# Masked attention: one more block of each group summed by an accumulating transfer, with resized tile pools

## The chip, the core and the metric

The kernel runs on one core of a Trainium2 chip. A core has TensorE (PE in the profile: matrix products and transposes), VectorE (DVE), ScalarE (ACT), GpSimd (POOL) and SyncE (SP), which issue in order, each from its own queue, and wait for each other by semaphores; 16 DMA engines move data. [...] The metric is the device time of one execution in microseconds (us), the median of several runs.

## The reference

Eight independent inputs (F = 8) of N = 2048 rows and C = 256 channels pass one attention layer with H = 8 heads of D = 32, under one mask adj, then layer norms and a small MLP:

```python
q, k, v = split(x @ w_qkv)                              # per head: [f, h, n, 32]
scores  = einsum('fnhd,fmhd->fhnm', q, k) / sqrt(32)
scores  = where(adj > 0, scores, -1e9)
attn    = softmax(scores, axis=-1)                      # exp(scores) / sum over m
t       = einsum('fhnm,fmhd->fnhd', attn, v)
y = layernorm(x + t); y = layernorm(y + mlp(y)); out = layernorm(x + y)
```

Everything is float32. Two sums over m (the keys) are wanted for every query and head: the sum of exp(score) times v, and the sum of exp(score) itself, the denominator. This document is about how the second is made.

## The kernel before

**Groups and slots.** The queries of an input are cut into four chunks of 512 (`qc`), the heads into two sets of four (`g`), the keys into 16 blocks of 128 (`mb`). A group is one `(f, qc, g)`; there are 8 x 4 x 2 = 64. One step of the main loop, here called a slot, handles one block of one group, so a group has 16 slots, the kernel has 1024, and one input ("frame") has 128. In slot t the loop issues, in this order:

- `advance(t)`: side work from the list `fill` (below);
- `exponentials(t+1)`: ScalarE turns the masked scores of the next block into exponentials in place (L237), a tile `p` of 128 x 2048 floats, that is 1 MB;
- `scores(t+2)`: TensorE computes the scores of the block after that (L230: four products of 32 rows each, side by side), and VectorE adds the mask on the way from PSUM into a new tile `p` (L233, two instructions);
- `values(t)`: TensorE multiplies block t's exponentials by v (L249), adding up in one PSUM bank over the 16 blocks;
- `add_up(t)`: the block is added to a partial sum for the denominator.

**The denominator.** Within a group the 16 tiles are reduced to four before TensorE sees them. Blocks 3, 6, 8, 11, 13, 15 are added into block 0's tile by GpSimd (L271, the list `POOLED`). Blocks 4, 7, 10 are added into block 1's tile and blocks 5, 9, 12 into block 2's by DMA transfers that read, add and write in SBUF (L268, the two chains of `MOVED`); GpSimd issues them, and before each it waits for the previous one of its chain to have landed. Block 14 (`ALONE`) stays as it is. `denominator` then multiplies each of the four tiles ("terms") by a matrix of ones (L310), one term at a time, in the order block 14, chain 1, chain 2, pooled; the PSUM result is the sum over keys. The last term is not issued before slot `t + SUM` (t = the group's last slot, SUM = 4). In the very last group blocks 13 and 15 are terms of their own (`ENDED`).

**Side work.** `denominator`, the projections (`project`: k and v of the next input, `ask`: its queries), transposes (`turn`) and the layer norms and MLP (`outcome`, `tail`, `feed_forward`) are Python generators in the list `fill`, with a start slot and a due slot. `advance` resumes them at build time: each slot earns 2200 units of credit (`STEP`), a product of four columns of 512 costs 2048, and the next piece is let in when the credit has 1024 (`UNIT`) or the piece is due. Most slots so carry one piece of side work on TensorE, between the values of one slot and the scores of the next; some carry two or none. `NEXT` lists, by slot of the frame, when the projections of the following work are started. All of it is one fixed program: the order on each engine is settled when it is built.

**Tile pools.** `pp` holds the 1 MB tiles `p` (11 of them), `kp` and `vp` the k and v tiles (12 each, a quarter of the size; 8 are in use for one input, the rest is room for the next), `qp` the query tiles (6). A new tile takes the buffer that was released first: in both programs, in nearly every group, the buffer of the new group's block 2 is that of block 10 of the group before (with 11 buffers) or of block 9 (with 12), and so on. VectorE's write at L233 waits for that release: for a block added by a transfer, until the transfer has landed; for one added by GpSimd, until the add is done; for a term, until its product with ones is done.

Of the kernel before, what the change touches and what calls it, by code (L numbers as in the profile page):

```python
# [61 lines left out]
def fast_path(ctx, tc, cst, x, adj, out, RS):  # L62
    nc = tc.nc
    F, N, C = x.shape
    NCK, TPC, MB = N // CH, CH // P, N // P
# [2 lines left out]
    dp = ctx.enter_context(tc.tile_pool(name="dp", bufs=1, space=bass.MemoryType.DRAM))  # L68
    mkp = ctx.enter_context(tc.tile_pool(name="mkp", bufs=MB // 2 + 1))
    ld = ctx.enter_context(tc.tile_pool(name="ld", bufs=LD))  # L70
    kp = ctx.enter_context(tc.tile_pool(name="kp", bufs=3 * NCK))
    qp = ctx.enter_context(tc.tile_pool(name="qp", bufs=6))
    vp = ctx.enter_context(tc.tile_pool(name="vp", bufs=3 * NCK))
    pp = ctx.enter_context(tc.tile_pool(name="pp", bufs=11))
    work = ctx.enter_context(tc.tile_pool(name="work", bufs=1))
    yp = ctx.enter_context(tc.tile_pool(name="yp", bufs=2))
    op = ctx.enter_context(tc.tile_pool(name="op", bufs=1))
# [14 lines left out]
    def transposes(ps, src, ident=ident):  # L92
        state["credit"] -= TURN
        for j, s in enumerate(src):
            nc.tensor.transpose(ps[:, j * P:(j + 1) * P], s, ident)
# [6 lines left out]
    def bank(dt=F32):  # L102
        shape = [P, CH] if dt == F32 else [P, 2, CH]
        if state["side"] is not None:
            i = 1 - state["side"]
            return ps_x[i].tile(shape, dt, name=f"x{i}")
        i = state["turn"]
        state["turn"] = (i + 1) % 5
        pool = ps_s[i] if i < 3 else ps_x[i - 3]
        return pool.tile(shape, dt, name=f"s{i}" if i < 3 else f"x{i - 3}")  # L110
# [4 lines left out]
    def take(shape, dt):  # L115
        live.pop(0)
        live.append(ld.tile(shape, dt, name="in"))
        return live[-1]
# [31 lines left out]
    def load_mask(f, qc, k):  # L150
        nc.sync.dma_start(words(mask_piece(f, qc, k)), MD[qc, k])
# [68 lines left out]
    PT, O, OT, RC = {}, {}, {}, {}  # L220

    def scores(item):
        f, qc, g, mb = item
        pt = PT[item] = pp.tile([P, 4, CH], F32, name="p")
        ps2 = [score_pair() for _ in range(2)]

        for half in (1, 0):
            for j in range(2):
                r = D * (2 * half + j)
                nc.tensor.matmul(ps2[half][:, j, :], KT[f, mb // TPC, g][r:r + D, (mb % TPC) * P:(mb % TPC + 1) * P],  # L230
                                 QT[f, qc, g][r:r + D, :], start=True, stop=True)
        for half, ps in enumerate(ps2):
            nc.vector.tensor_tensor(pt[:, 2 * half:2 * half + 2, :], ps,  # L233
                                    MK[f, qc, mb // 2][:, mb % 2, None, :].to_broadcast([P, 2, CH]), ALU.add)

    def exponentials(item):
        nc.scalar.activation(PT[item], PT[item], AF.Exp, scale=1.0 / math.sqrt(D))  # L237
# [17 lines left out]


    POOLED = (0, 3, 6, 8, 11, 13, 15)
    MOVED = ((1, 4, 7, 10), (2, 5, 9, 12))
    ALONE = 14

    ENDED = (13, 15)
    SUM = 4

    def add_up(item):
        f, qc, g, mb = item
        for chain in MOVED:
            if mb in chain[1:]:
                nc.gpsimd.dma_start(PT[f, qc, g, chain[0]], PT.pop(item), accum_op=ALU.add)  # L268
        if mb in POOLED[1:] and not ((f, qc, g) == items[-1][:3] and mb in ENDED):
            first = PT[f, qc, g, POOLED[0]]  # L270
            nc.gpsimd.tensor_tensor(first, first, PT.pop(item), ALU.add)  # L271
# [22 lines left out]

    def denominator(f, qc, g, ready):
        grp = (f, qc, g)
        terms = [PT.pop((f, qc, g, ALONE))] + [PT.pop((f, qc, g, chain[0])) for chain in MOVED + (POOLED,)]
        if (f, qc, g) == items[-1][:3]:
            terms[3:3] = [PT.pop((f, qc, g, b)) for b in ENDED]
        yield BANK  # L300
        ps = bank()
        for n, term in enumerate(terms):
            if n:
                yield MORE
            while n == len(terms) - 1 and state["now"] < ready:
                yield WAIT
            state["credit"] -= 4 * CH
            for h in range(4):
                r = D * h
                nc.tensor.matmul(ps[r:r + D, :], cst["ones"], term[:, h, :], start=(n == 0), stop=(n == len(terms) - 1))  # L310
        dT = op.tile([P, CH], F32, name="dT")
        nc.scalar.copy(dT, ps)
        yield 1
        yield BANK
        ps = bank()
        transposes(ps, [dT[:, j::TPC] for j in range(TPC)])
        if g == 0:
            RC[f, qc] = op.tile([P, TPC, H], F32, name="rc")
        rc = RC[f, qc]
        den = ps.rearrange("p (j c) -> p j c", c=P)[:, :, ::D]  # L320
        nc.vector.reciprocal(rc[:, :, 4 * g:4 * g + 4], den)
        nc.vector.tensor_tensor(RS[:, 0], RS[:, 0], den, ALU.add)
        nc.vector.tensor_tensor(RS[:, 1], RS[:, 1], den, ALU.min)
        if g == 1:
            begin = items.index((f, qc, g, LAST)) + SUM + 2
            start(begin, outcome(f, qc) if (f, qc) != (F - 1, NCK - 1) else finish(f, qc), begin)

    def outcome(f, qc):
        yield ROOM
        state["tails"] += 1  # L330
        xin = x[f, qc * CH:(qc + 1) * CH, :].rearrange("(p j) c -> p j c", p=P)
        y = yp.tile([P, TPC, C], F32, name="y")
        yield from divide(f, qc, y)
        nc.gpsimd.dma_start(y, xin, accum_op=ALU.add)
        begin = items.index((f, qc, 1, LAST)) + SUM + 2
        start(begin + 10, tail(f, qc, y, xin), begin + 26)
# [47 lines left out]
    def finish(f, qc):  # L384
        y = yp.tile([P, TPC, C], F32, name="y")
        xr, xb = state["rows"], take([P, TPC, C], F32)
        yield from divide(f, qc, y)
        nc.vector.tensor_tensor(y, y, xr, ALU.add)
        norm_halves(y)
        nc.vector.tensor_tensor(xb, xr, rows(cst["be2r"]), ALU.add)  # L390
        yield from feed_forward(y)
        z = y
        norm_halves(z)
        for h in range(0, TPC, 2):
            nc.vector.tensor_tensor(z[:, h:h + 2], z[:, h:h + 2], rows(cst["g2r"])[:, h:h + 2], ALU.mult)
            nc.vector.tensor_tensor(z[:, h:h + 2], z[:, h:h + 2], xb[:, h:h + 2], ALU.add)
        norm_halves(z)
        dst = out[f, qc * CH:(qc + 1) * CH, :].rearrange("(p j) c -> p j c", p=P)
        for h in range(0, TPC, 2):
            nc.sync.dma_start(dst[:, h:h + 2], z[:, h:h + 2])  # L400
# [40 lines left out]
    def start(t, gen, due):  # L441
        fill.append([t, gen, 1, due])
        fill.sort(key=lambda e: e[3])
# [50 lines left out]
    def ask(f, c):  # L494
# [2 lines left out]
        give(xT)  # L497

    NEXT = {1: [(turn, 0)], 2: [(ask, 1)], 20: [(turn, 1)], 34: [(ask, 2)], 40: [(project, 0, 0)], 50: [(turn, 2)],
            60: [(project, 1, 0)], 66: [(ask, 0), (ask, 3)], 72: [(turn, 3)], 80: [(project, 2, 0)], 92: [(project, 3, 0)],  # L500
            100: [(project, 0, 1)], 104: [(project, 1, 1)], 108: [(project, 2, 1)], 112: [(project, 3, 1)]}

    def begin():
        todo = deque((qc, c) for qc in range(NCK) for c in range(NCK))
# [47 lines left out]
    for t, (f, qc, g, mb) in enumerate(items):  # L552
        if g == 1 and mb % 2 and (f + 1 < F or qc + 1 < NCK):
            load_mask(f + (qc + 1) // NCK, (qc + 1) % NCK, mb // 2)
        for what, *which in NEXT.get(t % FRAME, []):
            to = f if what is ask and which[0] else f + 1
            if to < F:
                at = (0, 0, 0) if what is turn else (which[0], 0, 0) if what is ask else (0, which[1], which[0] * TPC)
                start(t, what(to, *which), t + 3 * MB if what is turn else items.index((to, *at)) - LEAD - 1)
        if t == len(items) - MB // 2:  # L560
            state["rows"] = take([P, TPC, C], F32)
            nc.sync.dma_start(state["rows"], x[f, qc * CH:(qc + 1) * CH, :].rearrange("(p j) c -> p j c", p=P))
        if t:
            advance(t)

        if t + 1 < len(items):
            exponentials(items[t + 1])
        if t + LEAD < len(items):
            nf, _, ng, nmb = items[t + LEAD]
            t0 = t  # L570
            while (nf, nmb // TPC, ng) not in V:
                advance(t0, finish=True)
                t0 += 1
            scores(items[t + LEAD])
        values(items[t])
        add_up(items[t])
        if mb == LAST:
            start(t + 2, denominator(f, qc, g, t + SUM), t + SUM + 4)
    t = len(items)
    state["side"] = None  # L580
    while fill:
# [238 lines left out]
```

## Time and profile before

| | |
|---|---|
| median of 3 runs | 3279.77 us (3279.57 to 3284.65) |
| the profiled execution's own time | 3279.45 us |
| its span, first to last instruction | 3277.3 us |
| mean granted TensorE clock | 0.983 |
| PE busy | 3112.2 us (95%) |
| DVE busy | 2737.7 us (84%) |
| POOL busy | 2591.2 us (79%) |
| ACT busy | 2438.8 us (74%) |

All later times come from one profiled execution. Its own time is 0.3 us from the median, and its span 2.2 us shorter than that time. An entry of the profile such as `L271 POOL TENSOR_TENSOR p<-p ... x382 | busy, mean | idle <-who` reads: the instruction of line 271 on GpSimd that writes a tile p from tiles p ran 382 times; then its busy time in us and mean duration in ns, then how long the engine sat idle right before it and which engine or transfer ended the wait. A busy PE is not necessarily an unstalled PE: a float32 product leaves two records, so a term of the denominator leaves eight at L310. The line numbers of the changed kernel are one lower from L259 on (L267 for the transfers' issue, L270 for GpSimd's adds, L309 for the products with ones).

### The profile page before, as it was taken

Reading aid. Unit: us, or ns where it says so; the run is one execution under the profiler, and the core shown is the slowest. Engines: PE = TensorE matmul, PEld = TensorE weight load, DVE = VectorE, ACT = ScalarE, POOL = GpSimd, SP = SyncE. Lnnn points to the kernel's source line nnn. Section 1 sums busy time; section 2 is a strip of 40 time slices with the busy share of each in tenths; the row PEclk is TensorE's granted clock in tenths of the full one; section 3 lists DMA queues with packets and bytes.
Section 4 is the critical chain, followed back from the end, with each engine's and each line's share of the span. In section 5 each row is a group of like instructions: output and inputs, shape, how many; then the busy total and the mean of one; then the engine's idle time right before and its main releaser. Section 6 shows DMA issues by size and latency. Waiting matters only on the chain. (4 is left out here: it accounts for less than half of the span.)

```text
span 3277.3 us, 68323 instructions
## 1 busy us (share of the span) xinstructions
PE 3112.2 (95%) x28948; PEld 979.2 (30%) x28948; DVE 2737.7 (84%) x3203; ACT 2438.8 (74%) x1937; POOL 2591.2 (79%) x1357
## 2 busy tenths in 40 slices
PE   7899999999999999999999999999999999999994
PEld 4222323233332223322233323323223323332221
DVE  4888988888888888888888888888888888878994
ACT  3677878777777777777777777777778777777773
POOL 0578888888878888788887888787888788878894
PEclk8899999999999999999999999999999999999997
DMA  9688779778879788788777879878779778877773
GB/s 318 145 177 189 162 179 200 176 178 197 175 174 207 171 189 185 157 197 200 180 173 173 184 179 213 173 167 197 175 179 198 175 172 201 175 164 163 164 161 77
DMA packets 153384, 591.57 MB, mean 181 GB/s; under 512 B 15056, under 2 KB 67792, under 8 KB 103920
## 3 DMA queue, kind: packets, MB, share of 16 engines
q0 software_dynamic: 64560, 435.85, 66.4%
q1 hardware_dynamic: 87696, 149.98, 13.1%
q8 instruction: 229, 3.75, 0.4%
q10 hardware_dynamic: 816, 1.31, 0.1%
q14 instruction: 83, 0.68, 0.1%
HBM read 146.67 MB, written 37.75 MB: 56 GB/s over the span
## 5 line engine op out<-in xcount | busy, mean ns | idle before, releaser
L233 DVE TENSOR_TENSOR p<-s,mask 128x1024 f32<-128x1024 f32 x2048 | 2409.4, 1218 | 395.7 <-PE s L230 190.0
L237 ACT ACTIVATE p<-p 128x2048 f32<-128x2048 f32 x1024 | 1956.2, 1910 | 554.8 <-DVE p L233 486.8
L271 POOL TENSOR_TENSOR p<-p 128x2048 f32<-128x2048 f32 x382 | 1824.0, 4776 | 268.5 <-ACT p L237 266.2
L230 PE MATMUL s<-qT,kT 32*128 32x512 f32 x8192 | 1173.5, 642 | 70.2 <-DVE p L233 65.7
L249 PE MATMUL x<-p,v 128*32 128x512 f32 x8192 | 1097.6, 608 | 14.0 <-ACT p L237 14.0
L268 POOL DMA_DIRECT2D p<-p x384 | 360.0, 955 | 289.4 <-DMA p<-p 94.4
L230 PEld LDWEIGHTS s<-qT,kT 32*128 32x128 f32 x8192 | 321.1, 183 | 679.0 <-DVE p L233 632.4
L249 PEld LDWEIGHTS x<-p,v 128*32 128x32 f32 x8192 | 161.5, 108 | 795.2 <-issue 294.2
L310 PE MATMUL x<-p,ones 128*32 128x512 f32 x2016 | 262.8, 598 | 4.3 <-POOL p L271 2.7
L54 PE MATMUL x<-in,wqkv 128*32 128x512 f32 x1888 | 244.0, 594 | 4.0 <-DMA in<-xd 4.0
L289 ACT ACTIVATE y<-y,nb,rs 128x256 f32<-128x256 f32 x372 | 219.1, 590 | 37.1 <-POOL nb L286 37.1
L278 DVE BATCH_NORM_STATS2 st<-y 128x6 f32<-128x256 f32 x372 | 155.0, 417 | 6.2 <-DMA y<-in_x_dram 6.2
L54 PE MATMUL x<-w2s,hT 128*32 128x256 f32 x2048 | 123.9, 383 | 3.2 <-DVE y L436 2.1
L54 PE MATMUL x<-turned,w1s 128*32 128x512 f32 x992 | 122.9, 592 | 0.2
L54 PEld LDWEIGHTS x<-wqkv,in 128*32 128x32 f32 x3584 | 102.3, 110 | 62.8 <-issue 59.8
L54 PE MATMUL x<-wqkv,in 128*32 128x128 f32 x3584 | 117.0, 273 | 0.0
L310 PEld LDWEIGHTS x<-p,ones 128*32 128x32 f32 x2016 | 65.7, 111 | 160.3 <-issue 145.8
L54 PEld LDWEIGHTS x<-in,wqkv 128*32 128x32 f32 x1888 | 61.3, 110 | 145.8 <-issue 112.1
L283 POOL TENSOR_TENSOR rs<-rs,mhalf 128x4 f32<-128x4 f32 x93 | 97.1, 1044 | 7.8
L54 PEld LDWEIGHTS x<-w2s,hT 128*32 128x32 f32 x2048 | 66.4, 111 | 77.0 <-issue 30.0
L414 POOL TENSOR_TENSOR y<-y,be1b2r 128x1024 f32<-128x1024 f32 x32 | 85.5, 2671 | 0.6
L355 POOL TENSOR_TENSOR y<-y,g2r 128x1024 f32<-128x1024 f32 x31 | 82.3, 2656 | 1.8 <-ACT y L289 1.8
(117 smaller groups left out, 1335.7 us busy)
## 6 DMA issues: line engine op xcount, KB each, us to landing
p<-p POOLq DMA_DIRECT2D x384, 1024.0 KB, 10.5
in<-xd SPq DMA_DIRECT2D x87, 512.0 KB, 10.6
mask<-md SPq DMA_DIRECT2D x248, 128.0 KB, 8.3
y<-in_x_dram POOLq DMA_DIRECT2D x62, 512.0 KB, 8.3
p<-in_adj_dram SPq DMA_DIRECT2D x16, 1024.0 KB, 9.5
out_dram<-y SPq DMA_DIRECT2D x31, 512.0 KB, 5.8
in<-in_x_dram SPq DMA_DIRECT2D x29, 512.0 KB, 15.3
xd<-in SPq DMA_DIRECT2D x28, 512.0 KB, 11.1
```

The lines of the kernel that those rows point to most:

```text
L54: nc.tensor.matmul(out[r:r + D], lhsT[:, r:r + D], rhs, start=start, stop=stop)
L230: nc.tensor.matmul(ps2[half][:, j, :], KT[f, mb // TPC, g][r:r + D, (mb % TPC) * P:(mb % TPC + 1) * P], QT[f, qc, g][r:r + D, :], start=Tr ...
L233: nc.vector.tensor_tensor(pt[:, 2 * half:2 * half + 2, :], ps, MK[f, qc, mb // 2][:, mb % 2, None, :].to_broadcast([P, 2, CH]), ALU.add)
L237: nc.scalar.activation(PT[item], PT[item], AF.Exp, scale=1.0 / math.sqrt(D))
L249: nc.tensor.matmul(O[grp][r:r + D, :], V[f, mb // TPC, g][:, mb % TPC, r:r + D], PT[item][:, h, :], start=(mb == 0), stop=(mb == LAST))
L268: nc.gpsimd.dma_start(PT[f, qc, g, chain[0]], PT.pop(item), accum_op=ALU.add)
L271: nc.gpsimd.tensor_tensor(first, first, PT.pop(item), ALU.add)
L278: nc.vector.bn_stats(st, t[:, j, :])
L283: nc.gpsimd.tensor_tensor(rs, rs, cst["mhalf"], ALU.pow)
L289: nc.scalar.activation(t[:, j, :], t[:, j, :], AF.Identity, bias=nb[:, j:j + 1], scale=rs[:, j:j + 1])
L310: nc.tensor.matmul(ps[r:r + D, :], cst["ones"], term[:, h, :], start=(n == 0), stop=(n == len(terms) - 1))
L414: nc.gpsimd.tensor_tensor(y, y, rows(cst["be1b2r"]), ALU.add)
```

## The change

- Block 14 is added by a transfer too: chain 1 becomes 1, 4, 7, 10, 14. `ALONE` is gone, `denominator` has three terms instead of four, and they come in the order chain 2 (2, 5, 9, 12), chain 1 (1, 4, 7, 10, 14), pooled. In the last group there are five terms instead of six.
- The denominator is started one slot later, at t + 3; the due slot and SUM are as before.
- `pp` has 12 tiles instead of 11. The room is taken from `kp` and `vp` (11 instead of 12 tiles) and `qp` (4 instead of 6).
- To fit the smaller pools, the first queries of the next input are asked for in slot 98 of the frame instead of 66, and the projections of slots 92, 100, 104, 108, 112 move to 100, 104, 108, 112, 116.

```diff
-    kp = ctx.enter_context(tc.tile_pool(name="kp", bufs=3 * NCK))
-    qp = ctx.enter_context(tc.tile_pool(name="qp", bufs=6))
-    vp = ctx.enter_context(tc.tile_pool(name="vp", bufs=3 * NCK))
-    pp = ctx.enter_context(tc.tile_pool(name="pp", bufs=11))
+    kp = ctx.enter_context(tc.tile_pool(name="kp", bufs=3 * NCK - 1))
+    qp = ctx.enter_context(tc.tile_pool(name="qp", bufs=4))
+    vp = ctx.enter_context(tc.tile_pool(name="vp", bufs=3 * NCK - 1))
+    pp = ctx.enter_context(tc.tile_pool(name="pp", bufs=12))
...
-    MOVED = ((1, 4, 7, 10), (2, 5, 9, 12))
-    ALONE = 14
+    MOVED = ((2, 5, 9, 12), (1, 4, 7, 10, 14))
...
-        terms = [PT.pop((f, qc, g, ALONE))] + [PT.pop((f, qc, g, chain[0])) for chain in MOVED + (POOLED,)]
+        terms = [PT.pop((f, qc, g, chain[0])) for chain in MOVED + (POOLED,)]
         if (f, qc, g) == items[-1][:3]:
-            terms[3:3] = [PT.pop((f, qc, g, b)) for b in ENDED]
+            terms[2:2] = [PT.pop((f, qc, g, b)) for b in ENDED]
...
-            60: [(project, 1, 0)], 66: [(ask, 0), (ask, 3)], 72: [(turn, 3)], 80: [(project, 2, 0)], 92: [(project, 3, 0)],
-            100: [(project, 0, 1)], 104: [(project, 1, 1)], 108: [(project, 2, 1)], 112: [(project, 3, 1)]}
+            60: [(project, 1, 0)], 66: [(ask, 3)], 72: [(turn, 3)], 80: [(project, 2, 0)], 98: [(ask, 0)], 100: [(project, 3, 0)],
+            104: [(project, 0, 1)], 108: [(project, 1, 1)], 112: [(project, 2, 1)], 116: [(project, 3, 1)]}
...
-            start(t + 2, denominator(f, qc, g, t + SUM), t + SUM + 4)
+            start(t + 3, denominator(f, qc, g, t + SUM), t + SUM + 4)
```

## The prediction, made before the changed kernel ran

> **What bounds the kernel now.** I read the page first (busy shares, queues, groups), then what the lines L233, L268 and L310 waited for, then the timeline at the end of two groups, then the stretches of one frame.
>
> ```profile
> PE 3112.2 (95%) x28948; PEld 979.2 (30%) x28948; DVE 2737.7 (84%) x3203; ACT 2438.8 (74%) x1937; POOL 2591.2 (79%) x1357
> ...
> q0 software_dynamic: 64560, 435.85, 66.4%
> q1 hardware_dynamic: 87696, 149.98, 13.1%
> ...
> L310 PE MATMUL x<-p,ones 128*32 128x512 f32 x2016 | 262.8, 598 | 4.3 <-POOL p L271 2.7
> ```
>
> Of the answers on single lines, two rows: how long L233 (VectorE) sat idle for transfers in all, with the number of times, and how long L268's transfers take from issue to landing.
>
> ```profile
>   DMA p<-p: 49.0, 35
> ```
> ```profile
> DMA to landing us min/median/max: 6.8/10.5/17.3
> ```
>
> TensorE is busy nearly all the time, so I measured slots: the distance from one L249 on TensorE to the next. The timeline of TensorE, VectorE and GpSimd at the end of group 28 (counted from 0; start, duration, instruction, wait before it):
>
> ```profile
> 1500.32 1.07 PE L249 MATMUL x<-p,v 128*32 128x512 f32 x8
> 1501.79 1.14 PE L230 MATMUL s<-qT,kT 32*128 32x512 f32 x8 [0.41 <-DVE p L233]
> 1502.86 1.07 PE L249 MATMUL x<-p,v 128*32 128x512 f32 x8
> 1503.74 1.04 PE L310 MATMUL x<-p,ones 128*32 128x512 f32 x8
> 1505.99 1.14 PE L230 MATMUL s<-qT,kT 32*128 32x512 f32 x8 [1.21 <-DVE p L233]
> 1507.06 1.07 PE L249 MATMUL x<-p,v 128*32 128x512 f32 x8
> 1507.94 1.04 PE L310 MATMUL x<-p,ones 128*32 128x512 f32 x8
> 1508.91 1.14 PE L230 MATMUL s<-qT,kT 32*128 32x512 f32 x8
> 1509.98 1.07 PE L249 MATMUL x<-p,v 128*32 128x512 f32 x8
> ```
> ```profile
> 1504.71 2.35 DVE L233 TENSOR_TENSOR p<-s,mask 128x1024 f32<-128x1024 f32 x2 [1.29 <-DMA p<-p]
> ```
> ```profile
> 1501.44 4.86 POOL L271 TENSOR_TENSOR p<-p 128x2048 f32<-128x2048 f32 x1
> 1505.95 2.68 POOL L357 TENSOR_TENSOR y<-y,be2r 128x1024 f32<-128x1024 f32 x1
> 1508.93 0.88 POOL L359 DMA_DIRECT2D y<-in_x_dram  x1 [0.30 <-POOL y L357]
> 1509.55 4.86 POOL L271 TENSOR_TENSOR p<-p 128x2048 f32<-128x2048 f32 x1
> ```
>
> The slot from 1507.06 to 1509.98 lasts 2.92 us: TensorE's own work, with one term. The slot from 1500.32 has no side work and lasts 2.54: VectorE sets it (two L233 in 2.35, and what stands between). The slot from 1502.86 would be 2.92 too but takes 4.20, because L233 waited 1.29 for a transfer to release its tile; 49.0 us in all at L233 are of this kind. On GpSimd the adds of blocks 13 (1501.44) and 15 (1509.55) close the group, with a layer norm's work between them; block 12's transfer went out at 1498.52. Two stretches, group 27 and 28, show the DMA share in the column before the last:
>
> ```profile
> 1408.00:1456.00 48.00, 46.63 (x424) 14.19 (x420) 41.06 (x50) 39.04 (x33) 39.07 (x24) 1.00 0.95 221
> 1456.00:1503.00 47.00, 46.59 (x456) 15.49 (x452) 42.91 (x50) 36.06 (x29) 37.74 (x19) 1.00 0.75 169
> ```
>
> **What the Trainium skill says.** "TensorE: Matmul & The Clock Gate", Part 3, The mechanism, says matmuls are strict FIFO. So a product with ones that waits holds up the scores and values behind it; the trace agrees, where a term waited for GpSimd (0.48 us at 1514.46) the next scores started that much later. "DMA: Bandwidth & Descriptors", Anatomy of one DMA, gives 2.0 us + bytes / 436e3: 4.4 us for 1 MB. These accumulating transfers took 6.8 at least; the measurement decides. The same page, Issuing engines are not separate DMA queues, says that all queues share the 16 engines; 66.4% + 13.1% and the page's DMA row agree. TensorE's page, Part 1, says an idle stretch lowers the matmul clock; in the trace the values at 1219.99, after a wait of 3.00 us for weights, took 1.94 us, not 1.07.
>
> **The change part by part.**
>
> *One term less per group.* 64 terms of 8 x 598 ns, four side by side: busy 1.04 us each, 66 us in all. But a slot that loses its only side work falls to 2.54, not to 2.92 - 0.97. The order of the two built programs gives the slots: those with two pieces (3.78 us, such as L54 beside L54 with 16 records) fall from 67 to 27, those with none rise from 63 to 86, those with one full piece (2.92) gain 17; the rest is unchanged. Sum: -40 x 3.78 + 17 x 2.92 + 23 x 2.54 = -151.2 + 49.6 + 58.4 = -43 us.
>
> *Twelve tiles.* The tile that block 2 of the next group takes is now block 9's, no longer block 10's, and so on: every release has a slot (2.9 us) more. Block 10's transfer landed at slot 15.7 of its group on average and 16.5 at the latest, against a write that wants it near 16.4; block 9's landed at 14.8 at the latest. So the 49 us at L233 go. What is late next is the term itself, below. At the start a twelfth tile may let a mask load go out earlier (VectorE waited 12.0 us for these at L528): 0 to 12 us gained, I take 0.
>
> *One transfer more per group.* Queue 0 spent 66.4% of 3277.3 = 2176 us on 435.85 MB, 5.0 us per MB, so 5.2 us of all 16 engines per tile of 1.05 MB. 64 more are 335 us, 10% of the span: the DMA share rises from about 80% to 90%, and in a stretch such as group 27's, 0.95 + 5.2/48 = 1.06, over the full. GpSimd pays 0.955 us per issue, 61 us; it idles 266 us at L271 for exponentials, so this lies beside, except that block 15's add slips 0.9 us.
>
> *The new wait.* Block 14's transfer is issued after block 13's add and whatever GpSimd has in between, that is where block 15's add starts now. It lands 7.0 us after that at best, and not before block 12's landing + 5.2, since they share the queue. TensorE asks for it as second term: the order puts the terms into slots 17, 18, 19 after the group's first in 43 groups, 18, 19, 20 in 20. Before, chain 1 ended with block 10, and block 12 was asked for one or two slots later.
> Group 28: issue 1509.55, landing 1516.5. Asked in slot 18: before 1510.87, less the wait that goes and shorter slots, 1510.0. TensorE stands 6.5 us. Group 27: issue 1459.6, landing 1466.6, asked at 1462.4 (in both, the slots from the group's seventh on are added up with the lengths of the new order): 4.2 us.
> The same for all eight groups of that frame (24 to 31; groups 2, 5, 6 of a frame have the later order): 1.2, 0, 3.4, 4.2, 6.5, 2.0, 4.7, 0.9, together 22.9 us; times 63/8 is 180 us. Behind the waiting product stand the scores of two blocks on, then VectorE, ScalarE and GpSimd, all idle with it. I estimate the bounds from the same rows: 40 us if block 14 is issued some two slots earlier than block 15's add started, 290 if mask and input traffic stretch 5.2 to 6.1 us per tile. The present waits at L310, 12.6 for GpSimd and 4 for transfers, are swallowed: -17. A slower clock after each wait is worth 0 to 30 us; I take 0.
>
> *Smaller kp, vp, qp and moved starts.* Slots 98 to 116 are each just past the last reader of the buffer that is wanted, so ScalarE's copies find it free: 0. SP carries the same number of loads; those of `ask` for the next input move 32 slots later, into stretches with a share of 0.78 to 0.89. L54 waited 4.0 us for such loads so far; 0 to 20, I take 0.
>
> *The end.* In the last group block 12's transfer was issued at 3212.58 and TensorE's terms waited until 3219.82. Block 14's now follows it and lands some 5.2 later, with the same three terms after it: +5.
>
> **Sum against the profiled execution:** 3279.5 - 43 - 49 - 17 + 180 + 5 = 3355; the median is 0.3 higher, 3356 us.
>
> **Rivals.**
> *The transfer lands in time.* If GpSimd, freed of the stalls of others, issues block 14 about two slots earlier, only 40 us of wait are left: 3279.5 - 43 - 49 - 17 + 40 + 5 = 3216 us, faster. For it: seven transfers take 7 x 5.2 = 36 us of a group's 48, and groups 25 and 31 wait hardly at all. It decides where block 14 lands before slot 18.3. Against it: block 12 alone lands at 17.4 on average and block 14 queues behind it.
> *Gain and waits cancel.* Waits near 104 us give 3279: no change.
> *The DMA engines become the bound.* With seven transfers per group the backlog in odd groups carries over: 290 us of wait, 3465. For it: the share of 1.06; against: even groups have room.
>
> **How the numbers follow.** Forecast 66%, 3356 us; DMA-bound 12%; in time 17%; cancelled 5%. Within 0.2% (6.6 us) is about what a measurement can't tell from no change. So slower 0.78, same 0.05, faster 0.17. The range, 3240 to 3430, leaves out some 11% of the fast side and 8% of the slow one.
>
> **What would show it.** L233's wait for DMA p<-p near 0; PE or its weight loads at L309 waiting for DMA p<-p for some 180 us in 40 to 60 pieces; 448 transfers, queue 0 near 75%; about 86 slots of 2.54. If L309's wait for transfers is below 60 us, the forecast is wrong and the kernel is faster; if it is above 250, the DMA engines are the bound.

## The result and the profile after

| | before | after |
|---|---|---|
| median of 4 runs, same chip | 3279.67 us (3272.23 to 3284.65) | 3526.36 us (3509.37 to 3531.26) |
| ratio, 95% interval | | 1.0745 (1.0704 to 1.0786) |
| profiled execution, its span | 3279.45, 3277.3 us | 3531.26, 3529.4 us |
| mean granted TensorE clock | 0.983 | 0.952 |

The direction was forecast, the size was not: 247 us slower, against 76 forecast and a range that ended at 3430. From the page of the kernel after (busy times, queues, and groups of instructions with busy time, mean ns, idle time before them and what ended it):

```profile
PE 3144.1 (89%) x28436; PEld 966.9 (27%) x28436; DVE 2731.9 (77%) x3203; ACT 2437.9 (69%) x1937; POOL 2643.7 (75%) x1421
...
q0 software_dynamic: 73776, 502.96, 71.3%
...
L230 PE MATMUL s<-qT,kT 32*128 32x512 f32 x8192 | 1205.3, 659 | 51.8 <-DVE p L233 42.5
L249 PE MATMUL x<-p,v 128*32 128x512 f32 x8192 | 1110.7, 615 | 0.8 <-ACT p L237 0.8
...
L309 PE MATMUL x<-p,ones 128*32 128x512 f32 x1512 | 226.1, 673 | 226.0 <-DMA p<-p 222.8
```

Two of these groups in the kernel before:

```profile
L230 PE MATMUL s<-qT,kT 32*128 32x512 f32 x8192 | 1173.5, 642 | 70.2 <-DVE p L233 65.7
L249 PE MATMUL x<-p,v 128*32 128x512 f32 x8192 | 1097.6, 608 | 14.0 <-ACT p L237 14.0
```

The work that the change removes from TensorE is gone (1512 records at L309 instead of 2016), and yet its busy time rose from 3112.2 to 3144.1 us: the same products take longer each (L230 642 to 659 ns, L249 608 to 615, the term 598 to 673). Idle time before the terms (TensorE stands; such a wait is called a stand below) went from 4.3 us to 226.0, nearly all of it waiting for the accumulating transfers. Queue 0 was busy for 71.3% of 3529.4 = 2516 us with 502.96 MB, 5.0 us per MB, the price it had before: its transfers did not become dearer.

I counted, slot by slot, how much later each term started than it does right behind the values of its slot, summed over 63 groups (the last group apart): before 10 us in all; after 28, 213 and 13 us for the first, second and third term, 254 together. The second term waits over 0.5 us in 59 of 63 groups. The timeline of TensorE at the end of group 24 (start, duration, instruction, wait before it) shows one:

```profile
1404.87 1.07 PE L249 MATMUL x<-p,v 128*32 128x512 f32 x8
1412.51 1.94 PE L309 MATMUL x<-p,ones 128*32 128x512 f32 x8 [6.57 <-DMA p<-p]
1414.38 2.09 PE L230 MATMUL s<-qT,kT 32*128 32x512 f32 x8
1416.39 1.07 PE L249 MATMUL x<-p,v 128*32 128x512 f32 x8
```

and GpSimd's timeline shows why:

```profile
1393.50 1.19 POOL L267 DMA_DIRECT2D p<-p  x1
...
1400.96 1.50 POOL L358 DMA_DIRECT2D y<-in_x_dram  x1
1401.54 1.80 POOL L267 DMA_DIRECT2D p<-p  x1
1402.10 5.82 POOL L270 TENSOR_TENSOR p<-p 128x2048 f32<-128x2048 f32 x1
```

Block 12's transfer goes out at 1393.50, a half-size transfer of x for the layer norm at 1400.96, and block 14's at 1401.54, right behind it on the same queue. TensorE asks for the second term at about 1405.8 and gets it at 1412.5, some 11 us after the issue. The term and the scores behind it then run at 1.94 and 2.09 us, not at the 1.06 and 1.14 of the slot before.

One more new wait, in TensorE's timeline, at slot 13 of the third group of a frame:

```profile
1494.69 1.06 PE L249 MATMUL x<-p,v 128*32 128x512 f32 x8
1505.10 1.12 PE L95 MATMUL x<-ident,in 128*128 128x128 f32 x4 [9.35 <-DMA in<-in_x_dram]
1506.15 2.09 PE L230 MATMUL s<-qT,kT 32*128 32x512 f32 x8
```

The transposes of the next input (`turn`) reach the engine before their load has landed: 28.9 us in six waits; before there were none. VectorE's wait for transfers at L233, 49.0 us before, is gone.

### The profile page after: what moved, and what is told of

Read it like the earlier page. It is cut to its first block, busy times and chain, and to the rows that moved or that the text cites. A ratio compares the mean times of both kernels' runs of the same rounds, so it can differ in the third digit from the quotient of the medians.

```text
span 3529.4 us, 67539 instructions
## 1 busy us (share of the span) xinstructions
PE 3144.1 (89%) x28436; PEld 966.9 (27%) x28436; DVE 2731.9 (77%) x3203; ACT 2437.9 (69%) x1937; POOL 2643.7 (75%) x1421
## 3 DMA queue, kind: packets, MB, share of 16 engines
q0 software_dynamic: 73776, 502.96, 71.3%
## 5 line engine op out<-in xcount | busy, mean ns | idle before, releaser
L233 DVE TENSOR_TENSOR p<-s,mask 128x1024 f32<-128x1024 f32 x2048 | 2409.0, 1218 | 660.8 <-PE s L230 335.3
L270 POOL TENSOR_TENSOR p<-p 128x2048 f32<-128x2048 f32 x382 | 1881.5, 4928 | 314.3 <-ACT p L237 312.1
L230 PE MATMUL s<-qT,kT 32*128 32x512 f32 x8192 | 1205.3, 659 | 51.8 <-DVE p L233 42.5
L249 PE MATMUL x<-p,v 128*32 128x512 f32 x8192 | 1110.7, 615 | 0.8 <-ACT p L237 0.8
L267 POOL DMA_DIRECT2D p<-p x448 | 484.5, 1098 | 449.0 <-ACT p L237 255.4
L230 PEld LDWEIGHTS s<-qT,kT 32*128 32x128 f32 x8192 | 327.8, 187 | 683.8 <-DVE p L233 565.7
L309 PE MATMUL x<-p,ones 128*32 128x512 f32 x1512 | 226.1, 673 | 226.0 <-DMA p<-p 222.8
L249 PEld LDWEIGHTS x<-p,v 128*32 128x32 f32 x8192 | 162.6, 109 | 806.5 <-issue 302.3
L311 ACT COPY dT<-x 128x512 f32<-128x512 f32 x63 | 36.9, 585 | 303.4 <-PE x L309 303.4
L288 ACT ACTIVATE y<-y,nb,rs 128x256 f32<-128x256 f32 x372 | 219.3, 590 | 9.1 <-POOL nb L285 9.1
L309 PEld LDWEIGHTS x<-p,ones 128*32 128x32 f32 x1512 | 44.2, 117 | 373.8 <-DMA p<-p 268.5
L356 POOL TENSOR_TENSOR y<-y,be2r 128x1024 f32<-128x1024 f32 x31 | 89.2, 2879 | 0.0
```

Of the source, the lines that this page charges most:

```text
L249: nc.tensor.matmul(O[grp][r:r + D, :], V[f, mb // TPC, g][:, mb % TPC, r:r + D], PT[item][:, h, :], start=(mb == 0), stop=(mb == LAST))
L288: nc.scalar.activation(t[:, j, :], t[:, j, :], AF.Identity, bias=nb[:, j:j + 1], scale=rs[:, j:j + 1])
```

## The experiments

Three theories. **A**: the denominator is asked for too early, so TensorE stands for block 14's transfer; the work itself is cheap. **B**: the DMA engines are the bound, seven transfers a group being too many. **C**: the smaller pools and moved starts (the queries asked for in slot 98 and so on) cost much of it. Each kernel was timed beside the kernel before on the same chip (three chips in all; the medians of the kernel before were 3279.3 to 3280.6 us there). "Measured" gives the median, then its ratio to the kernel before with the 95% interval; waits, shares and clocks come from one profiled execution of each kernel. "Term waits" are counted as above, for the first, second and third term. The edits are against the changed kernel unless said otherwise.

**late5: the start two slots later.** Nothing else changes, so all 448 transfers stay.

```diff
-            start(t + 3, denominator(f, qc, g, t + SUM), t + SUM + 4)
+            start(t + 5, denominator(f, qc, g, t + SUM), t + SUM + 4)
```


> The changed kernel with the denominator started at t + 5 instead of t + 3, so that its three terms stand in slots 20, 21, 22 of the group in most groups, after block 14's transfer has landed (slot 18.9 on average in the changed kernel). Same 448 transfers. Theory A (TensorE stands at the product with ones until block 14's transfer lands, and its clock is lower after each stand): the wait of L309 for transfers falls from 223 us to below 30, and the time to 3210 to 3270 us. Theory B (the DMA engines are overloaded by 64 more transfers): the time stays above 3430. Theory C (the smaller kp, vp, qp and the moved starts cost it): above 3430 too, with the wait elsewhere.

Measured 3213.81 us, 0.9786 (0.9766 to 0.9805). Term waits 1.8, 36.4 and 1.8 us, clock 0.983, no wait for the input's load. From its page:

```profile
q0 software_dynamic: 73776, 502.96, 77.4%
...
L309 PE MATMUL x<-p,ones 128*32 128x512 f32 x1512 | 198.7, 597 | 32.7 <-DMA p<-p 32.7
```

Queue 0's share is higher than in the changed kernel: the same transfers in less time. B falls as the explanation of the loss. The wait for transfers at L309, 32.7 us, is slightly more than expected; the terms stand in slots 19, 20, 21 in 47 of 63 groups, one earlier than the expectation says.

**alone12: pools and starts without the fifth transfer.** Against the kernel before, only the pool sizes and `NEXT` change.

```diff
-    pp = ctx.enter_context(tc.tile_pool(name="pp", bufs=11))
+    pp = ctx.enter_context(tc.tile_pool(name="pp", bufs=12))
...
-            60: [(project, 1, 0)], 66: [(ask, 0), (ask, 3)], 72: [(turn, 3)], 80: [(project, 2, 0)], 92: [(project, 3, 0)],
...
+            60: [(project, 1, 0)], 66: [(ask, 3)], 72: [(turn, 3)], 80: [(project, 2, 0)], 98: [(ask, 0)], 100: [(project, 3, 0)],
...
```


> The changed kernel's pools and moved starts, but block 14 is a term of its own again (four terms in the old order, denominator started at t + 2, 384 transfers). Theory A: 3220 to 3290 us, the 49 us of wait at L233 for transfers gone, and against that up to 33 us of TensorE standing for an input load before its transposes. Theory B: about the same, 3230. Theory C: above 3400.

Measured 3246.72 us, 0.9899 (0.9881 to 0.9917). L233 waits 2.5 us for transfers. The twelfth tile with everything it needed gains 33 us; C falls.

**chain11: the fifth transfer without the pools.** The mirror image: `MOVED`, the order of the terms and t + 3 as in the changed kernel, pools and `NEXT` as before.

```diff
-    MOVED = ((1, 4, 7, 10), (2, 5, 9, 12))
-    ALONE = 14
+    MOVED = ((2, 5, 9, 12), (1, 4, 7, 10, 14))
...
-            start(t + 2, denominator(f, qc, g, t + SUM), t + SUM + 4)
+            start(t + 3, denominator(f, qc, g, t + SUM), t + SUM + 4)
```


> The kernel before with block 14 in the chain alone: three terms in the new order, denominator at t + 3, but 11 tiles p, the old kp, vp, qp and the old starts. Theory A: 3430 to 3530 us, with over 200 us of L309's wait for transfers; without the wait for input loads before the transposes it is some 30 us under the changed kernel, and L233's wait of up to 49 us returns in part. Theory B: above 3450. Theory C: below 3330.

Measured 3512.5 us, 1.0714 (1.0692 to 1.0737). Term waits 19.6, 183.4 and 12.3 us, clock 0.949. So nearly the whole loss sits in this part: 233 of 247 us. The two parts do not simply add up (33 us gained in alone12 and 233 lost here would make 200): while the terms wait, the larger pool shows no gain, and L233's wait for transfers is down to 9.2 us even with 11 tiles. A miss inside it: the wait for the input's load is there too, 35.1 us in five pieces, although the starts are the old ones. It does not come from the moved starts, as I had thought.

**drop14: no block 14 in the denominator at all.** This kernel leaves block 14 out of the sum (its denominators lack that block); order, start and pools are those of the changed kernel.

```diff
-    MOVED = ((2, 5, 9, 12), (1, 4, 7, 10, 14))
+    MOVED = ((2, 5, 9, 12), (1, 4, 7, 10))
...
+        if mb == 14:
+            PT.pop(item)
```


> The changed kernel with block 14 left out of the denominator: neither a transfer nor a term, so the denominators lack one block of 16. It shows what three terms and twelve tiles are worth without the transfer. Theory A: 3200 to 3250 us (block 12's transfer is still asked for early, at slot 17, so some 30 us of wait remain). Theory B: below 3260 too. Theory C: above 3400.

Measured 3300.19 us, 1.0062 (1.0044 to 1.0080): 50 us above the expected span. Term waits 63.6, 5.5 and 0.2 us, clock 0.976, and 28.7 us of waits for the input's load. The first term, chain 2 with block 12, is asked for from slot 17 on, and block 12's transfer lands at slot 17.4 on average. So the new order and start are too early for block 12 as well. In the changed kernel the first term waits less, 28 us: its slots are longer with the stands in them, and block 12 lands at slot 17.0.

**late4: one slot later.** `start(t + 4, ...)`, to have a point between.

> The changed kernel with the denominator started at t + 4, half way to late5. If TensorE stands only for the part of the transfer's landing that its own order leaves open, each group waits up to one slot (2.9 us) less than in the changed kernel: of 213 us of wait at the second term some 70 to 100 remain, the lower clock after long stands mostly goes, and the time is 3250 to 3320 us. If the DMA engines were the bound, it would stay near 3500.

Measured 3316.24 us, 1.0107 (1.0090 to 1.0124). Term waits 4.4, 89.4 and 7.5 us, clock 0.972, 13.4 us for the input's load.

**last14: the chain with block 14 as the last term, start at t + 3.**

```diff
-        terms = [PT.pop((f, qc, g, chain[0])) for chain in MOVED + (POOLED,)]
+        terms = [PT.pop((f, qc, g, chain[0])) for chain in (MOVED[0], POOLED, MOVED[1])]
```


> The changed kernel with the terms in the order chain 2, pooled, chain 1, so that block 14's transfer is asked for last, one slot later, and the pooled sum (GpSimd's add of block 15 ends at slot 17.8 on average) one slot earlier. Theory of the wait: as late4 but for a few groups that now wait for GpSimd, 3280 to 3360 us, and the wait moves to the third term. If the order of the terms does not matter: near 3526.

Measured 3363.28 us, 1.0243 (1.0224 to 1.0261), 3 us above the expected span. Term waits 47.2, 49.9 and 34.5 us: the wait for block 14 shrinks to 34.5, but the pooled sum, which ends with block 15's add on GpSimd, is now asked for too early, and block 12 still is.

**ydelay: the half-size transfer out of the way.** In `tail`, the transfer of x (L358) is issued three slots later, so that it stands behind block 14's transfer and not before it.

```diff
-        yield 1
+        yield 4
```


> The changed kernel with the transfer that adds x to y before the last layer norm issued three slots later, so that in every second group it goes out after block 14's transfer instead of just before it on the same queue. If block 14 lands late because it queues behind that half megabyte, the even groups wait 2.5 us less each, some 60 us in all, and the time falls to 3430 to 3480 us. If it only waits for GpSimd's issue and for block 12: above 3510.

Measured 3466.25 us, 1.0565 (1.0527 to 1.0604): 60 us faster than the changed kernel. Block 14's transfer takes 9.08 us from issue to landing instead of 11.45, block 12's 8.8 instead of 10.6 (means over groups 8 to 55), and the term waits fall from 254 to 163 us. What lies ahead on the queue is a good part of the landing time.

**warm3: a product instead of a stand.** The first term's product is written three times more, each time over the one before, ahead of the second term. TensorE gets some 2.4 us more work per group in the place where it stands.

```diff
+            for again in range(4 if n == 1 and grp != items[-1][:3] else 1):
+                first = n == 1 and again < 3 and grp != items[-1][:3]
...
```


> The changed kernel with the first term's product with ones written three times more, right before the second term, so that TensorE works for 2.6 us of the time in which it stood (the denominators stay as they are). 63 x 2.6 = 163 us of work go into 213 us of wait; where a group waited less than that, the rest is added, some 35 us. If the lower clock after a stand costs the 70 us that the longer matmuls of the changed kernel show, the time falls by 15 to 50 us all the same; if it costs nothing it rises by 20 to 40 us.

Measured 3518.25 us, 1.0727 (1.0698 to 1.0756). From the waits of this kernel (the product with ones is its line 311):

```profile
PE x L311 <- DMA p<-p: 96.2, 35, 5.8
```

The product's busy time rises by 378.9 - 226.1 = 153 us and this wait falls by 222.8 - 96.2 = 127; the time moves by 8 us downward, with intervals that overlap. L230's mean is 650 ns instead of 659, the clock 0.970 instead of 0.952. Apart from the added product TensorE was busy some 36 us less (3144.1 + 153 against 3261.4 on this kernel's page), so the products behind a shorter stand are faster. The time fell between the two expected spans, so how much of it the clock costs this run does not show.

**chain11late5: chain11 with t + 5.** Does the old pool cost anything once the term waits are gone?

> The kernel before with block 14 in the chain, the new order of terms and the start at t + 5, but 11 tiles and the old kp, vp, qp and starts. It tells what the twelfth tile is worth once TensorE no longer waits. If a tile's release a slot earlier is worth the 49 us that L233 waited for transfers in the kernel before: 3240 to 3275 us, with 30 to 60 us of such waits back. If the tile is worth nothing here: 3205 to 3225, as late5.

Measured 3238.14 us, 0.9874 (0.9852 to 0.9896), 24 us above late5, just below the expected span. VectorE waits 80.3 us (46 times) for transfers at L233, against 12.3 in late5. The twelfth tile, with the smaller pools and moved starts that it needs, is worth 24 us here.

**late5last14: both edits.** t + 5 and the order chain 2, pooled, chain 1.

> The changed kernel with the start at t + 5 and the order chain 2, pooled, chain 1. Block 14's transfer lands at slot 20.0 on average in late5 and is asked for there at 20.3, with 40 us of wait left over in 23 groups; asked for at 21.3 nearly all of it goes: 3165 to 3200 us. If the 40 us are not the order's: 3214.

Measured 3184.95 us, 0.9708 (0.9687 to 0.9730): the lowest time of this study, below late5 and last14 alone. Its page:

```profile
PE 3046.4 (96%) x28436; PEld 960.3 (30%) x28436; DVE 2731.8 (86%) x3203; ACT 2445.9 (77%) x1937; POOL 2652.6 (83%) x1421
...
q0 software_dynamic: 73776, 502.96, 78.2%
...
L309 PE MATMUL x<-p,ones 128*32 128x512 f32 x1512 | 197.0, 592 | 3.2 <-DMA p<-p 2.4
```

The same records as in the changed kernel, 98 us less busy: a term takes 592 ns per record instead of 673, the stand before it is 2.4 us instead of 222.8, and queue 0 moves the same bytes at a share of 78.2%.

**late6: `start(t + 6, ...)`.** The old order, one slot later still.

> The changed kernel with the start at t + 6. The second term stands in slot 21 in most groups, so its wait falls below 10 us; tiles of the three terms come free one slot later, which has room. 3175 to 3215 us. If a later start costs elsewhere (the next group's work bunched, tiles late): above 3225.

Measured 3189.52 us, 0.9721 (0.9699 to 0.9742). TensorE waits 0.6 us for transfers at L309, and VectorE 21.9 us at L233, against 12.3 in late5: the tiles come free a slot later. Later start and later chain reach nearly the same time; their intervals overlap.

**late5both: late5last14 with the edit of ydelay.**

> As late5last14, with the transfer of x before the last layer norm three slots later as in ydelay. With nothing left to wait for at the terms, freeing the queue is worth little: within 10 us of late5last14. If the queue itself holds up other work: 20 us or more faster.

Measured 3277.58 us, 0.9998 (0.9987 to 1.0008): 93 us slower than without the edit, a clear miss. From its waits:

```profile
DVE y L435 <- PE x L54: 115.2, 44, 12.3
ACT y L288 <- POOL nb L285: 112.4, 27, 8.3
```

With the transfer of x three slots later, the layer norm behind it comes later; its small operations on GpSimd (`nb`) stand behind 5 us adds, and ScalarE waits at L288 for them with the exponentials of later blocks behind it (in late5last14 that wait is 27.3 us). This is read from the waits; no run took it apart. ydelay has the same wait at L288, 72.2 us against 9.1 in the changed kernel, so its 60 us are probably what remains after such a cost.

**Read together.** Only the start differs in this series:

| start | t + 3 | t + 4 | t + 5 | t + 6 |
|---|---|---|---|---|
| time, us | 3526.4 | 3316.2 | 3213.8 | 3189.5 |
| term waits, us | 254 | 101 | 40 | 2 |
| clock | 0.952 | 0.972 | 0.983 | 0.985 |

From t + 3 to t + 5 the terms wait 214 us less and the kernel is 312.6 us faster. With them went 28.9 us of waits for the input's load; without these, 284 us are left, and each us of term wait cost about 1.3 us. The rest fits the clock: TensorE's busy time fell by 86.5 us as well (3144.1 to 3057.6 on late5's page), and not all of that need show in the time. A holds, with an addition on the clock.

## Why the prediction was wrong

The sum of the prediction was 3279.5 - 43 - 49 - 17 + 180 + 5.

- *Slots, -43.* The kinds of slots came out as forecast: 86 without side work, 27 with two pieces. The size fits roughly as well: late6, whose terms hardly wait, is 57 us below alone12, whose four terms wait 20 us by the same count.
- *Twelve tiles, -49.* The wait at L233 is gone, but that was VectorE's idle time and not TensorE's, and its disappearance is worth less than its length: 33 us in alone12, 24 us between chain11late5 and late5, and nothing that shows between chain11 (3512.5) and the changed kernel (3526.4).
- *Old waits at L310, -17.* Too large: of its 12.6 us for GpSimd, 9.9 are idle time of the weight loads, and TensorE itself stood 2.7; by the count of starts the terms were 10 us late in all.
- *The new wait, +180.* **This is the first of two steps that failed.** Measured: 213 us at the second term, 254 at all three. "It lands 7.0 us after that at best, and not before block 12's landing + 5.2" took the best case as the usual one, and left out of the queue what does not belong to the two chains: the transfer took 11.45 us from issue to landing on average. Put on the issues and landings of the changed kernel's own trace, that rule is 2.7 us too early on average: 4.4 in the 23 groups in which the transfer of x goes out less than 3 us before block 14's, 1.7 in the other 40. Better figures were at hand: the row quoted for L268 has a median of 10.5 beside its minimum of 6.8, and GpSimd's timeline of group 28 shows the transfer of x at 1508.93, just ahead of the place where block 14's would go (with that transfer out of the way, in ydelay, it is 9.08 us).

  A second error went the other way: block 14's transfer goes out earlier before the question than forecast, 4.8 us in group 28 where 0.5 was taken, 8.8 in group 27 where 2.8 was. So it is luck that 180 came as near as it did. In the eight groups that were worked out singly the forecast was 22.9 us and the trace has 23.2, but not in the same groups: 6.8 for 1.2 in group 24, none for 3.4 in group 26.

  The eight do not stand for all either: in the four inputs after theirs the second term waits 27 to 36 us each; why, was not looked into. And 28 us at the first term and 13 at the third were taken as nothing, although block 12 was asked for earlier too. The wait stayed below the 290 us of the upper bound, but not for the reason given there.
- *A slower clock, +0 of 0 to 30.* **The second step that failed, by as much again.** Busy time at L230 rose by 31.8 us, at L249 by 13.1; the 189 terms took 226.1 us instead of 189 x 1.043 = 197. That is 74 us; by TensorE's whole busy time, against late5last14 with the same records, it is 98. In the records, from the second term's start to the next values is 2.1 us on average where the term had waited under 2 us (19 groups), 2.8 where it had waited 2 to 4 us (23 groups), and 3.8 where it had waited over 4 us (21 groups). "TensorE: Matmul & The Clock Gate", Part 1, The HAM clock gate, puts the fall of the clock at an idle window of about 3.4 us and the return at as much busy time; the trace agrees: its record of the granted clock has 45 stretches at half speed, 43 of them 3.4, 6.8 or 10.2 us long, where the kernel before has 11. The prediction named this page and gave an example (1.94 us for 1.07), forecast waits over 4 us in three of eight groups, and still took nothing: 24 groups with two products, each 0.87 us longer as in that example, make 42 us.
- *Moved starts, +0 of 0 to 20.* The input's load costs 29 us, but chain11 has it with the old starts and late5 and alone12 don't have it with the new ones. It goes with kernels that start the terms at t + 3 and, with 13.4 us, with late4; what in their side work brings the transposes forward was not taken apart.
- *The end, +5.* From the last values to the end: 66.6 us before, 73.6 after, +7.

With the measured terms the sum is 3279.5 - 43 - 49 - 17 + 254 + 74 + 29 + 7 = 3535 us against 3531 in the profiled execution. That they meet is in part luck: with the sizes found above for the tile (24 to 33, or nothing), the old waits (10) and the clock (98), the sum is 50 to 85 us too high, so some terms count the same time twice; which, the runs don't say.

*The rivals.* The time came nearest to the rival with the DMA engines as the bound (3465), yet its mechanism is wrong: late5 moves the same bytes in 3214 us, at 5.0 us per MB throughout. So the mark set for it, over 250 us of waits at L309 (222.8 on the page, 254 as counted here), does not mark it: that wait grows as well when the question comes too early. The rival in which the transfer lands in time was worked out at 3216 us for 40 us of wait; late5, with just 40 us, took 3214. That close a match is luck, as its -49 and -17 are too large. It named GpSimd's earlier issue as the lever; no run tried that, and what the runs show to decide is TensorE asking later.

## What to carry to other kernels

When an in-order engine asks for a transfer, count from the issue with the transfer's usual time and with everything that stands ahead on the queue, and then add what the stand does to the engine's clock: here about 1.3 us were lost for each us waited. Where the asking side has slack, first move the question: two slots later turned +7.4% into -2.1%, and with the late chain asked for last into -2.9%. Move other things out of the way only with an eye on what waits for them; the same small shift gained 60 us in one version and cost 93 in another.

## What was not expected of the hardware

- An accumulating transfer of 1 MB within SBUF takes 5.0 us of the queue's time per MB in all kernels, at shares of 66% to 78%, while issue to landing takes 7 to 13 us on average, depending on the block; ydelay shows that what stands ahead on the queue is a part of it.
- Products after a stand of over 4 us run at about half speed, in group 24 for some 4 us (1.94 and 2.09 us instead of 1.06 and 1.14), and work put into the stand was nearly free here: 153 us more of products in warm3 left the time as it was.
